# A fused conditional transformer block: the adapter takes two batches at once in halves of the matrix array, and its last bias is added to the tokens by GpSimd

## The chip, the cores and the metric

The kernel runs on one core of one Trainium2 chip. A core has five engines that each work through their own queue in order: TensorE (PE in the profile; its weight loads are shown as PEld), VectorE (DVE), ScalarE (ACT), GpSimd (POOL) and SyncE (SP, which here only issues transfers). Sixteen DMA engines serve all queues. The metric is the device time of one execution in microseconds. The kernel before was timed three times: 921.53, 926.4 and 923.14 us, so its median is 923.14 us.

## The reference, cut to what matters

Four layers follow one another for 16 batches of 256 tokens with 256 features, all in float32. The change touches the first of them, the adapter, which picks one of 16 expert matrices per batch:

```python
# layer 0: adapter (A = 64), x is [16, 256, 256]
hidden = gelu(x @ down_W.T + down_b)                     # [b, 256, 64]
expert = hidden @ expert_W[domain_id].T + expert_b[domain_id]
hidden = where(valid, expert, hidden) + domain_emb[domain_id]
x      = layernorm(hidden @ up_W.T + up_b + x) * gamma + beta
# layer 1: x = ln(x) * (1 + scale(t)) + shift(t); q, k, v; 16 heads of 16
scores = q @ k.T / 4 + attention_bias ; masked ; softmax ; @ v ; @ Wo ; + x
x      = x + (gelu2(ln(x) @ W1 + b1) @ W2 + b2)          # 256 -> 1024 -> 256
# layer 2: one of three small networks, chosen per batch; x = ln(x + net(x))
# layer 3: one step of a Fokker-Planck equation: products with stencils, relu
```

The attention bias (`side` in the kernel) has 16 x 16 x 256 x 256 elements, 64 MB, and is the largest input by far.

## The kernel before, in words

The tokens of a batch lie as 128 partitions by two chunks by 256 features. Every layer is written as a Python generator that goes through the batches and yields where it must wait: `prepare` (the adapter and the first two normalisations), `project` (q, k, v), `weigh` (scores and exponentials, four heads at a time, a "quad"), `attend` (the weights turned by the PE and multiplied with v), `enter` and `feed` (the feed-forward part), `end` (the chosen network), and `step` (the stencils). A small planner, `Flow`, keeps an estimated clock for each engine and for each of seven PSUM banks, and always continues the generator that is ready and has the lowest due time. The due time of a generator starts at a number given in `flow.add` and grows with the PE time that its steps claim, divided by a claimed PE time per batch. So the planner writes out, once, when the program is built, the order of all instructions on all engines; on the chip each engine follows its own list, and waits on semaphores where the data is not there yet.

Of the adapter, `prepare` issues this for each batch b:

- L523: two matmuls that multiply the transposed tokens with `w_down` (the contraction over 256 features in two halves of 128); the result `a_h` has 64 partitions (the adapter's width) by 256 tokens. A float32 matmul leaves two records on the PE, two passes of 256 columns.
- L525: gelu with the bias, by ScalarE, 64 partitions. ScalarE holds one set of function tables at a time, so the gelu needs a table load, and the next exponential needs another one.
- L540 and L542: one 64 x 64 matmul with the batch's expert matrix `e_w`; VectorE adds the chosen expert bias and embedding and writes `hid`, a tile of 65 partitions whose last row is all ones.
- L549 and L550: two matmuls of `hid` with `up`, which has 65 rows: the last one is `up_b`, so the row of ones adds the bias. VectorE adds the result to the tokens.
- Then mean and variance (L407, L408 on VectorE and four small instructions on GpSimd, L411 to L415), the normalisation with gamma and beta (for batch 0 on VectorE, L437 and L440; later on with two GpSimd instructions, L446 and L447), again mean and variance, and the normalised tile `c_ln` (L423 or L428), which `project` turns and multiplies with the weights of q, k and v.

One transfer per batch (L244) brings tokens and transposed tokens together, 512 KB into one of two buffers, and one (L295) brings the expert matrix, whose index SyncE first reads from a tile. Both are issued by `prepare` during the batch before. SyncE's queue also holds the loads of the attention bias: 1 MB per quad in four transfers (L307), three buffers. From batch 1 on, the mask is added to a loaded quad by a GpSimd transfer that accumulates (L508).

At the start, matmuls on zeros (`idle`, L222) stand between the adapter's steps of batches 0 and 1. In the first quads there is no earlier batch whose later layers could fill the PE.

## Time and profile before

| What | Value |
|---|---|
| median of three runs | 923.14 us |
| profiled execution | 919.35 us, of which the span is 917.5 us |
| TensorE clock granted, mean over the span | 0.990 |
| PE / DVE / ACT / POOL busy | 885.9 / 639.5 / 568.6 / 357.1 us |
| adapter matmuls (records, busy): L523, L540, L549 | 64, 18.1 us; 32, 10.3 us; 64, 16.8 us |
| transfers | 163.05 MB, mean 178 GB/s |

The profile comes from one execution. "Busy" is the time in which an engine had at least one instruction of the group under way. Matmuls overlap, so the mean duration of one (380 ns for 256 columns) is longer than the distance from one start to the next; where a price is wanted, the distance between the starts of neighbouring groups in the timeline is the better figure. Idle time is shown with what ended it. A line number is a line of the kernel.

### The profile page before, as it was taken

The page shows a single profiled execution, that of the slowest core. Times are in us where ns is not written, and L with a number is a line of the kernel's source. Part 1 is how long each engine was busy: PE and PEld are TensorE (multiplying, and loading weights), DVE is VectorE, ACT ScalarE, POOL GpSimd, SP SyncE. Part 2 cuts the span into 40 slices and gives each one's busy share as a digit, 9 for nine tenths or more (in the row PEclk, how much of TensorE's full clock was granted, in tenths as well). Part 3 has the DMA queues.
Part 4 walks back from the last instruction along what each step waited for, and adds up shares of the span by engine and source line. Part 5 has one row for each costly group of instructions (what it writes and reads, how often), then busy time and mean ns, then how long its engine had stood idle before and what let it go on. Part 6 is the DMA issues. An engine that isn't in the chain of part 4 may idle for free. (4 is left out here: it accounts for less than half of the span.)

```text
span 917.5 us, 18282 instructions
## 1 busy us (share of the span) xinstructions
PE 885.9 (97%) x6180; PEld 698.2 (76%) x6180; DVE 639.5 (70%) x2110; ACT 568.6 (62%) x1561; POOL 357.1 (39%) x500
## 2 busy tenths in 40 slices
PE   8899998999999999999999999999999999999997
PEld 3567675887777887778788777877887788778885
DVE  6677767767785767677686777768777785766343
ACT  2576667667665766758576675847667576656330
POOL 2233329142632616245261614526161543422331
PEclk8999999999999999999999999999999999999999
DMA  9389887776596767949676794967678486861010
GB/s 292 102 241 326 231 217 193 203 206 184 139 239 171 185 184 183 228 127 242 170 176 179 189 247 114 238 171 170 178 204 208 124 206 173 213 149 42 1 41 24
DMA packets 126555, 163.05 MB, mean 178 GB/s; under 512 B 12455, under 2 KB 86266, under 8 KB 126458
## 3 DMA queue, kind: packets, MB, share of 16 engines
q0 software_dynamic: 31680, 62.92, 34.1%
q1 hardware_dynamic: 93568, 96.92, 32.5%
q10 hardware_dynamic: 1209, 1.99, 0.7%
q8 instruction: 52, 0.85, 0.4%
q14 instruction: 46, 0.37, 0.1%
HBM read 94.69 MB, written 4.19 MB: 108 GB/s over the span
## 5 line engine op out<-in xcount | busy, mean ns | idle before, releaser
L718 ACT ACTIVATE c_pr<-c_sc,c_mx 128x256 f32<-128x256 f32 x512 | 255.1, 500 | 179.6 <-DVE c_mx L707 178.7
L707 DVE CUSTOM_DVE_ANT_0 c_sc<-c_s,side 128x256 f32<-128x256 f32 x512 | 194.4, 417 | 28.3 <-ACT e_o L1096 7.7
L454 PE MATMUL c_pt<-ident,c_pr 128*128 128x128 f32 x1024 | 143.5, 278 | 7.0 <-ACT c_pr L718 5.2
L454 PEld LDWEIGHTS c_pt<-ident,c_pr 128*128 128x128 f32 x1024 | 116.6, 142 | 34.6 <-ACT c_pr L718 12.7
L462 DVE COPY c_pts<-c_pt 128x512 f32<-128x512 f32 x183 | 122.8, 685 | 27.7 <-PE c_pt L454 27.4
L508 POOL DMA_DIRECT2D side<-neg x60 | 80.8, 1355 | 143.9 <-DMA side<-in_side 70.4
L411 POOL TENSOR_SCALAR rs<-mv 128x2 f32<-128x2 f32 x64 | 14.2, 221 | 293.6 <-DVE mv L408 291.7
L873 PE MATMUL d_f<-d_ht,w 128*128 128x256 f32 x512 | 121.4, 381 | 0.1
L903 PE MATMUL d_o<-w,d_z 128*128 128x256 f32 x512 | 116.0, 380 | 0.0
L903 PEld LDWEIGHTS d_o<-w,d_z 128*128 128x128 f32 x512 | 95.0, 190 | 12.3 <-issue 0.4
L873 PEld LDWEIGHTS d_f<-d_ht,w 128*128 128x128 f32 x512 | 92.8, 190 | 11.9 <-issue 0.9
L718 ACT ACTIVATION_READ_ACCUMULATOR c_pr<-c_sc,c_mx 128x1 f32 x512 | 96.1, 188 | 0.0
L689 PE MATMUL c_s<-c_kt,c_qz 32*128 32x256 f32 x1024 | 76.6, 401 | 0.8 <-DVE c_mx L707 0.4
L772 PE MATMUL c_c<-c_pts,c_va 128*32 128x256 f32 x1024 | 72.0, 387 | 3.3 <-DVE c_pts L462 2.9
L689 PEld LDWEIGHTS c_s<-c_kt,c_qz 32*128 32x128 f32 x1024 | 47.9, 184 | 23.5 <-issue 15.8
L892 ACT ACTIVATE d_f<-d_z 128x512 f32<-128x512 f32 x64 | 38.2, 597 | 28.5 <-DVE d_z L889 27.7
L772 PEld LDWEIGHTS c_c<-c_pts,c_va 128*32 128x32 f32 x1024 | 27.5, 109 | 33.4 <-issue 16.1
L911 DVE SCALAR_TENSOR_TENSOR y<-d_o,y 128x256 f32<-128x256 f32 x32 | 13.6, 424 | 55.5 <-PE d_o L903 55.5
L889 DVE TENSOR_SCALAR d_z<-d_f,cols 128x256 f32<-128x256 f32 x102 | 44.5, 477 | 10.7 <-PE d_f L873 9.9
L412 POOL TENSOR_TENSOR rs<-rs,inv_sqrt 128x2 f32<-128x2 f32 x64 | 46.0, 719 | 5.3
L464 ACT COPY c_pts<-c_pt 128x512 f32<-128x512 f32 x73 | 41.7, 572 | 8.8 <-PE c_pt L454 7.7
L896 DVE SCALAR_TENSOR_TENSOR d_z<-d_f,d_z 128x512 f32<-128x512 f32 x64 | 43.1, 673 | 3.5 <-ACT d_f L892 3.5
(152 smaller groups left out, 1602.2 us busy)
## 6 DMA issues: line engine op xcount, KB each, us to landing
side<-in_side SPq DMA_DIRECT2D x256, 256.0 KB, 5.6
side<-neg POOLq DMA_DIRECT2D x60, 1024.0 KB, 8.4
x<-in_x SPq DMA_DIRECT2D x16, 512.0 KB, 5.6
d_w<-in_W_branch SPq DMA_DIRECT2D x16, 512.0 KB, 6.4
out<-e_o SPq DMA_DIRECT2D x15, 256.0 KB, 4.9
w<-in_W SPq DMA_DIRECT2D x2, 1024.0 KB, 7.5
d_bout<-in_bl_branch SPq DMA_DIRECT2D x16, 128.0 KB, 5.8
grids<-in_grids SPq DMA_DIRECT2D x1, 1792.0 KB
```

The costliest lines, as they stand in the source:

```text
L412: nc.gpsimd.tensor_tensor(rs, rs, inv_sqrt, ALU.pow)
L454: nc.tensor.transpose(ps[:, k, c * P : (c + 1) * P], src[:, c, k * P : (k + 1) * P], ident)
L462: nc.vector.tensor_copy(dst, ps)
L508: nc.gpsimd.dma_start(out=sides[m].rearrange("p (h c) k -> p h (c k)", h=HB), in_=negs[m // 4].rearrange("p c k -> p (c k)").unsqueeze(1). ...
L689: nc.tensor.matmul(ps[i][:, c, :], qz[rows32, par, half, c * P : (c + 1) * P], k_t[rows32, half, :], start=b > 0, stop=b > 0 or c == NC - 1,)
L707: nc.vector.tensor_tensor_reduce(out=sc[:, c, :], in0=ps[i][:, c, :], in1=sb[:, i * NC + c, :], scale=-1.0, scalar=3.0e38, op0=ALU.add, op ...
L718: nc.scalar.activation(pr[:, c, :], sc[:, c, :], AF.Exp, bias=mx[:, c : c + 1], scale=-1.0, accum_out=sums[:, c, h : h + 1],)
L772: nc.tensor.matmul(ps_c[32 * i : 32 * i + 32, :], va[:, k, 4 * half + i, 2 * par : 2 * par + 2, :].rearrange("p e d -> p (e d)"), turned[i ...
L873: nc.tensor.matmul(ps_f[:, i, :], w1[:, k, f * P : (f + 1) * P], h_t[:, k, :], start=k == 0, stop=k == NC - 1,)
L889: nc.vector.tensor_scalar(z[:, i, :], ps_f[:, i, :], b1[:, f : f + 1], None, ALU.add)
L896: nc.vector.scalar_tensor_tensor(z, ps_f, 1.0, z, ALU.add, ALU.mult)
L903: nc.tensor.matmul(ps_o, us[f // 2][:, f % 2, c * P : (c + 1) * P], w2[:, f, :], start=f == 0, stop=f == NF - 1,)
```

## The change

The adapter becomes a generator of its own, `adapt`, that goes through eight pairs of batches. Batch 2p uses one half of the array and batch 2p + 1 the other:

- The first product puts the two batches into two halves of the array's columns: both contract over 128 rows and write 64 partitions each, 0 to 63 and 64 to 127 of one tile `p_h`.
- One gelu over 128 partitions serves both batches.
- The expert product of one batch uses rows 0 to 63 and columns 0 to 63, that of the other rows 64 to 127 and columns 64 to 127; one VectorE instruction adds the bias for both.
- The last product uses rows 0 to 63 for one batch and rows 64 to 127 for the other, with `up` held twice, and writes two PSUM banks. Its bias is no longer a row of `up`: it arrives, spread over all partitions, at the end of `rows_a`, and GpSimd adds it to the tokens beforehand (`biased`). The row of ones is gone.

The tokens and the transposed tokens now arrive by transfers of their own (three buffers of 256 KB, and one of 512 KB for a pair, in two transfers). `prepare` waits until its batch is adapted; the other steps of it stay. Two of the `idle` matmul groups, one of 256 columns and one of 512, are gone. The numbers in the `flow.add` calls are others.

```diff
-    def load_x(b):
-        xs[b] = xp.tile([P, NC, 2 * D], F32, name=f"x{b}", tag="x")
+    def load_turned(p):
+        arrives["t", p] = flow.clock["PE"] + 9.0 if p else 0.0
+        xts[p] = xp.tile([P, 2, NC, S], F32, name=f"xt{p}", tag="xt", bufs=1)
+        for i in range(2):
+            nc.sync.dma_start(out=xts[p][:, i], in_=chunked(t["x_t"][2 * p + i]))
+    def load_x(b):
+        arrives["x", b] = flow.clock["PE"] + 7.0 if b > 1 else 0.0
+        xs[b] = xp.tile([P, NC, D], F32, name=f"x{b}", tag="x", bufs=3)
         nc.sync.dma_start(out=xs[b], in_=chunked(t["x"][b]))
-    load_x(0)
-    up = load("up", t["up"], [A + 1, D])
+    load_turned(0)
+    up = load("up", t["up"], [2 * A, D])
...
-    def load_expert(b):
-        e = nc.sync.value_load(e_idx[0:1, b : b + 1], min_val=0, max_val=E + 1)
-        w = xp.tile([A, A], F32, name=f"e_w{b}", tag="e_w")
-        nc.sync.dma_start(out=w, in_=t["expert_W"][bass.ds(e, 1)].rearrange("e a o -> a (e o)"))
-        e_ws[b] = w
+    def load_expert(p):
+        e_ws[p] = xp.tile([2 * A, A], F32, name=f"e_w{p}", tag="e_w")
+        for i in range(2):
+            e = nc.sync.value_load(e_idx[0:1, 2 * p + i : 2 * p + i + 1], min_val=0, max_val=E + 1)
+            nc.sync.dma_start(
+                out=e_ws[p][i * A : (i + 1) * A, :],
+                in_=t["expert_W"][bass.ds(e, 1)].rearrange("e a o -> a (e o)"),
+            )
...
-    rows_a = load("rows_a", rows(t["rows_a"]), [P, 4 * D])
-    ln0_g, ln0_b, bv, bo = (rows_a[:, i * D : (i + 1) * D] for i in range(4))
+    rows_a = load("rows_a", rows(t["rows_a"]), [P, 5 * D])
+    ln0_g, ln0_b, bv, bo, up_b = (rows_a[:, i * D : (i + 1) * D] for i in range(5))
...
+    load_expert(0)
+    load_x(0)
     load_mask(0)
-    load_expert(0)
     load_side(0)
     load_x(1)
-    load_expert(1)
...
+    def biased(b):
+        x = xs[b]
+        nc.gpsimd.tensor_tensor(x, x, up_b.unsqueeze(1).to_broadcast([P, NC, D]), ALU.add)
+        flow.pool(1.35, arrives["x", b])
+        done.add(("x", b))
+
+    def adapt():
+        for p in range(B // 2):
+            yield lambda: p in e_ws
+            yield arrives.get(("t", p), 0.0)
+            parts = [slice(i * A, (i + 1) * A) for i in range(2)]
+            w, xt = e_ws.pop(p), xts.pop(p)
+            ps_h = misc(f"p_h{p}", [2 * A, S])
+            for k in range(NC):
+                for i in range(2):
+                    nc.tensor.matmul(
+                        ps_h[parts[i]], w_down[:, k, :], xt[:, i, k, :], start=k == 0, stop=k == NC - 1
+                    )
+            h1 = xp.tile([2 * A, S], F32, name=f"a_h1{p}", tag="a_h1", bufs=1)
+            nc.scalar.activation(h1, ps_h, AF.Gelu, bias=columns("down_b"))
+            at = free(f"p_h{p}", flow.act(0.47, flow.pe(1.0), "gelu"))
+            if p == 0:
+                expert_bias()
+            yield at
+            if p == 0:
+                spread_mask(0)
+                for b in range(2):
+                    biased(b)
+            ps_e = misc(f"p_e{p}", [2 * A, S])
+            for i in range(2):
+                nc.tensor.matmul(ps_e[parts[i]], w[parts[i]], h1[parts[i]], start=True, stop=True)
+            h2 = xp.tile([2 * A, S], F32, name=f"a_h2{p}", tag="a_h2", bufs=1)
+            nc.vector.tensor_scalar(h2, ps_e, e_add[:, p : p + 1], None, ALU.add)
+            at = free(f"p_e{p}", flow.dve(0.4, flow.pe(0.5)))
+            if p and 2 * p + 2 < B:
+                load_turned(p + 1)
+                load_expert(p + 1)
+            if p:
+                yield lambda: ("x", 2 * p + 1) in done
+            yield at, 2
+            if p == 0:
+                timestep()
+                idle(256)
+            ps_u = [misc(f"p_u{2 * p + i}", [P, NC, D]) for i in range(2)]
+            for c in range(NC):
+                for i in range(2):
+                    nc.tensor.matmul(
+                        ps_u[i][:, c, :], h2[parts[i], c * P : (c + 1) * P], up[parts[i]], start=True, stop=True
+                    )
+            at = flow.pe(1.0)
+            for b in (2 * p, 2 * p + 1):
+                x = xs[b]
+                nc.vector.tensor_tensor(x, ps_u[b % 2], x, ALU.add)
+                adapted[b] = free(f"p_u{b}", flow.dve(0.7, at))
+                done.add(("adapt", b))
+                yield 0.0, 0
+
     def prepare():
         for b in range(B):
-            w = e_ws.pop(b)
-            xx = xs.pop(b)
-            x, xt = xx[:, :, :D], xx[:, :, D:]
...
+            yield lambda: ("adapt", b) in done
+            x, at = xs.pop(b), adapted.pop(b)
+            yield at, 0
+            flow.spent += 0.75
+            if b + 2 < B:
+                load_x(b + 2)
+                if b == 0:
+                    load_turned(1)
+                    load_expert(1)
+            if b == 1:
+                choose()
             stat, at = take_stats(f"0_{b}", x, at)
...
             lns[b] = ln, normalized(ln, x, stat, b == 0)
+            flow.spent += 1.5
+            if b + 2 < B:
+                biased(b + 2)
             done.add(("normal", b))
...
-    flow.add(prepare(), -2.56, 2.25)
-    flow.add(project(), -0.82, 5.7)
+    flow.add(adapt(), -3.55, 1.2)
+    flow.add(prepare(), -2.34, 2.25)
+    flow.add(project(), -0.88, 5.7)
...
-    flow.add(enter(), -0.26, 0.44)
+    flow.add(enter(), -0.11, 0.44)
...
-    flow.add(end(), 2.77, 3.95)
-    flow.add(step(), 4.22, 7.0)
+    flow.add(end(), 2.86, 3.95)
+    flow.add(step(), 4.31, 7.0)
```

## The prediction

> **What bounds the kernel now.** I read the page first, then busy time by stretches of the span, then the waits of the PE, then the timeline around adapter groups and of the first 32 us.
>
> ```profile
> span 917.5 us, 18282 instructions
> PE 885.9 (97%) x6180; PEld 698.2 (76%) x6180; DVE 639.5 (70%) x2110; ACT 568.6 (62%) x1561; POOL 357.1 (39%) x500
> ...
> 10.00:20.00 10.00, 9.09 (x32) 5.01 (x32) 7.15 (x29) 4.59 (x7) 1.99 (x6) 0.76 1.08 363
> ...
> 120.00:160.00 40.00, 35.39 (x263) 26.01 (x265) 30.84 (x106) 27.95 (x79) 25.39 (x33) 0.96 0.79 199
> ...
> 520.00:560.00 40.00, 39.97 (x283) 32.61 (x278) 29.83 (x102) 27.10 (x77) 14.45 (x20) 1.00 0.77 192
> ```
>
> The columns of a stretch are its length, busy time of PE, PEld, DVE, ACT and POOL (with counts), granted clock, DMA share and GB/s. From 160 to 800 us the PE is busy practically without a break (39.97 of 40 us) while DVE has 10 us and POOL 25 us to spare: there, PE time taken out of the queue is time won. Of 31.6 us in which the PE is idle (917.5 - 885.9), about 4 lie before 30 us, 12 from 30 to 160 us, 9 at the end. So two questions decide: how much PE time the pairing removes after the start, and what it does to the start.
>
> The timeline gives the price of the adapter's groups as the distance from a group's start to the next start:
>
> ```profile
> 215.15 1.08 PE L523 MATMUL a_h<-x,w_down 128*64 128x256 f32 x4
> 216.16 0.33 PE L454 MATMUL c_pt<-ident,c_pr 128*128 128x128 f32 x1
> ...
> 220.50 0.64 PE L540 MATMUL a_e<-a_h,e_w 64*64 64x256 f32 x2
> 221.07 0.33 PE L454 MATMUL c_pt<-ident,c_pr 128*128 128x128 f32 x1
> ...
> 184.70 1.15 PE L689 MATMUL c_s<-c_kt,c_qz 32*128 32x256 f32 x16
> 185.78 0.33 PE L454 MATMUL d_t<-ident,d_ln 128*128 128x128 f32 x1
> ...
> 218.91 1.07 PE L772 MATMUL c_c<-c_pts,c_va 128*32 128x256 f32 x16
> 219.91 0.33 PE L454 MATMUL c_pt<-ident,c_pr 128*128 128x128 f32 x1
> ```
>
> Four records of `a_h` take 1.01 us, two of `a_e` 0.57; `a_u` takes 0.96 before a score group (183.74 to 184.70) and 0.87 before a full one (235.14 to 236.01). Sixteen records of scores (four row strips) take 1.08 us and sixteen of `c_c` (four column strips of one bank) 1.00 us: as long as four. Strips do run side by side here, with both passes of float32.
>
> **Change, term 1: PE time after the start.** Per batch before: 1.01 + 0.57 + 0.92 = 2.50 us. Per pair after: `p_h` four slots of two column halves, 1.01 (nearest row `a_h`; `c_c` says 1.00); `p_e` two slots, 0.57; `p_u` four slots of two row halves, 1.08 (nearest row: scores). Together 2.66, against 5.00. I count from the first score group, 30.33 us before. Before, batch 1's `a_u` and batches 2 to 15 come after it: 0.96 + 14 x 2.50 = 36.0 us. In the changed order pair 1's `p_h` and `p_e` stand before batch 0's q, so what follows is its `p_u` and pairs 2 to 7: 1.08 + 6 x 2.66 = 17.0 us. Gain 19.0 us. Bounds: 20.2 if a pair costs one batch's smallest sum (2.45); 16 if halves overlap less well than strips (a half slot of 0.22 us lost at each of some 14 places); nothing if they don't overlap at all (a rival below).
>
> A rule speaks against part of it. The rows show four column strips in one bank at once, but no two row strips in one bank, as `p_e` has them. The Trainium skill, "TensorEngine Tiling (Array Packing)", Restrictions and Gotchas, says that different row tiles cannot access one PSUM bank at the same time. By it `p_e` would cost two slots of 0.22 us more per pair, 2.6 us in six pairs, and the sum at the end would be 915.2.
>
> **Term 2: the start.** The lines that matter:
>
> ```profile
> 11.10 0.48 SPq L295 DMA_DIRECT2D e_w<-in_expert_W  x1
> ...
> 15.09 2.79 SPq L307 DMA_DIRECT2D side<-in_side  x4
> ...
> 19.76 1.97 PE L523 MATMUL a_h<-x,w_down 128*64 128x256 f32 x4
> ...
> 20.54 0.73 DVE L423 TENSOR_SCALAR c_ln<-x,mv,rs 128x256 f32<-128x256 f32 x2 [0.80 <-POOL rs L412]
> ...
> 24.05 0.30 PEld L597 LDWEIGHTS c_q<-c_xt,w_qkv 128*128 128x128 f32 x2 [0.54 <-ACT c_xt L583]
> 24.06 2.02 PE L597 MATMUL c_q<-c_xt,w_qkv 128*128 128x256 f32 x8
> ```
>
> Before, batch 0 reaches q at 24.06, after VectorE wrote `c_ln` at 20.54. In the changed program's order VectorE's queue has the bias addition of pair 1 (it waits for `p_e` of pair 1) directly ahead of batch 0's `c_ln`, and the PE's queue has `p_h` and `p_e` of pair 1 ahead of batch 0's turn `c_t`. Pair 1 needs the transposed tokens of batches 2 and 3, and SyncE issues those after three quads of side data (the last ends at 15.09 + 2.79 = 17.9 before). Ahead of them now stand one more index read and expert transfer (0.8 + 0.5), `x` of batch 0 and the mask (0.4 each), less the expert transfer that stood at 11.10 (1.3): third quad at 18.7, `x` of batch 2 and the two turned loads by 19.9. A load of tokens lands 5.6 us later (median): 25. By bytes: 7.55 MB stand in the two queues up to that load, 6.70 MB had moved by 22.9 us before (292 GB/s, first slice of the page), and 0.35 MB per us was the rate while the DMA was full: 25.3. I take 25.0. Then `p_h` at the slow clock, 1.97 (the row at 19.76; warm 1.08): 27.0; to `p_e` another 0.9 with the gelu (8.60 to 10.57 less 1.08); to VectorE's addition 0.68 (23.33 to 24.01), it takes 0.5; `c_ln` from about 29.1; to q 2.2 more (0.93, then `c_t` 0.64, then `c_xt` 0.61 by the starts at 22.80, 23.44, 24.05): 31.3, or 7.3 later than before.
>
> After the idle matmuls, which end near 20, the PE now stands still until 25. The row at 19.76 shows what a low clock does (1.97 for 1.01; granted 0.76 in that stretch). Whether q and k follow at the low clock costs 0 to 1.9 us (their eight matmuls of 1.89 doubled); 1.2 is taken, as the row nearest is cold. The Trainium skill, "TensorE: Matmul & The Clock Gate", Part 1, says that one idle window of about 3.4 us halves the clock and about 3.4 us of work restore it; by it 1.7 would be lost, and the sum would end at 913.1.
>
> Start: 7.3 + 1.2 = 8.5 us lost. Bounds: 4.9 (tokens at 23.5, every matmul warm) and 11 (landing 6.9 us, the longest shown, and 1.9 for the clock). GpSimd's additions for batches 0 and 1 (its queue has both ahead of the first `rs`) wait for `x` of batch 1, issued near 12, landed near 18 (6.0 to 6.8 in that stretch): `rs` of batch 0 moves from 15.7 to about 21, still ahead of the 29 above, so it costs nothing; if the turned tokens came early it would be next, with `c_ln` near 25.
>
> **Term 3: what lies beside.** GpSimd: 16 additions of 128x512 at 1.27 to 1.60 us (L447, L446): 20 to 26 us in a queue with 560 us idle. Behind each stand the `rs` of the next normalisation and the mask transfers (L508); before, that queue waited 70.4 us for side data alone, and VectorE's reductions waited 4.1 us for the masked data. Cost 0; with that cover gone, 26; no gain, since nothing leaves that queue but two memsets. ScalarE loses 8 gelus of 0.47 and 16 table loads of 1.28 (62 to 46), VectorE 8 additions of 0.47; the planner also shifts evictions between the two, and by the rows DVE ends 14 and ACT 12 us lower. The PE waited 5.2 us for exponentials, 2.9 for turned weights (all before 160 us) and 7.7 for `e_t`; at the start less adapter work is now left to fill such gaps, later less evicting delays them: -5 to +4, taken as 0. SyncE issues 16 more transfers of 0.42, 6.7 us, beside 393 us of waiting for side buffers: 0 after the start. The two `idle` groups (0.7 and 1.3 us) leave a stretch where the PE waits anyway: 0.
>
> **Sum.** 919.35 - 19.0 + 8.5 = 908.9 for an execution like the profiled one, whose span has 1.85 us around it. The median stands 3.79 us above that execution: 912.6.
>
> **Rivals.**
> - *The halves don't overlap.* Then a pair costs 5.0, the gain is nil and the start still costs 8.5: 931.6. For it: no 64-wide pair in the trace. Against: strips of both kinds overlap. 0.04.
> - *The start costs little*, because tokens land early and batch 1's earlier projection fills gaps in which the PE waited for exponentials: 923.14 - 19 = 904. 0.14.
> - *Another engine becomes the bound for part of it*: half of the 19 us turns into PE waiting for DVE or ACT. For it: DVE at 30 of 40 us, waits by 120 to 160 us. 923.14 - 9.5 + 8.5 = 922.1. 0.10.
> - *Slower: GpSimd blocks.* An addition waits for its `x`, whose load stands behind a side load that waited up to 17.0 us for its buffer; the mask transfer behind it comes late, and with it the scores' reduction on VectorE. It decides from 10.5 / 14 = 0.75 us of PE wait per addition; at 1.6 us each the time is 912.6 + 22 = 935. Against: `x` is loaded one batch earlier than it is added, some 50 us. 0.09.
>
> **Numbers.** The forecast itself has 0.63. Its own range, by the bounds: 919.35 - 20.2 + 4.9 - 5 = 899 and 919.35 - 16 + 11 + 4 = 918, plus 3.8: 903 to 922. It holds the second rival and, stretched to 923, the third; together 0.8 or a little more, since some of the first 0.63 may fall outside. Half a per cent, 4.6 us, is about what a measurement tells from no change: faster means under 918.5. Faster: 0.58 + 0.14 + 0.02 = 0.74; same 0.05 + 0.07 + 0.02 = 0.14; slower 0.04 + 0.07 + 0.01 = 0.12.
>
> **What would show it.** Right: `p_h`, `p_e`, `p_u` groups of eight, four and eight records with two starting together, 1.0, 0.6 and 1.1 us to the next group; first q near 31 us, with `c_ln` just after pair 1's bias; PE busy near 863 us; 39.9 of 40 us in the middle. Wrong: records one after the other; q near 25; new PE waits that lead to `x` on GpSimd; middle stretches under 39 us.

## The result and the profile after

The changed kernel takes 923.22 us (median of 12 runs, 917.59 to 927.28) where the kernel before takes 923.86 (12 runs, 920.27 to 926.4): a ratio of 0.999 with a 95% interval of 0.9966 to 1.0014. The forecast was 912.6, so nothing is seen of the 10.5 us that the change should have given. The spread of the runs goes with the granted clock of TensorE: its mean was 0.985 in the run of 917.59 us and 0.974 in that of 927.28, and 0.011 of the span is 10 us. The profiled execution of the changed kernel took 923.92 us, about its median; that of before lies 4.5 us under its own. A difference between the two traces is therefore some 5 us too large.

The head of the page, and stretches of the span in the columns of the prediction (length, busy time of PE, PEld, DVE, ACT and POOL with counts, granted clock, DMA share, GB/s), of the changed kernel:

```profile
span 922.1 us, 18224 instructions
PE 882.4 (96%) x6180; PEld 692.1 (75%) x6180; DVE 627.8 (68%) x2078; ACT 556.5 (60%) x1561; POOL 376.6 (41%) x514
...
10.00:20.00 10.00, 7.63 (x29) 4.93 (x28) 3.54 (x14) 4.61 (x7) 4.04 (x3) 0.60 1.06 335
20.00:30.00 10.00, 7.95 (x20) 3.31 (x20) 3.73 (x13) 0.47 (x1) 4.14 (x9) 0.50 0.62 189
30.00:40.00 10.00, 8.41 (x24) 6.29 (x23) 5.20 (x22) 2.17 (x5) 1.35 (x4) 0.54 0.27 83
...
280.00:320.00 40.00, 37.78 (x275) 29.69 (x274) 26.23 (x94) 25.52 (x74) 14.96 (x18) 1.00 0.76 191
520.00:560.00 40.00, 39.85 (x282) 31.83 (x283) 27.36 (x91) 28.35 (x76) 17.60 (x23) 1.00 0.74 188
720.00:760.00 40.00, 37.40 (x286) 29.37 (x285) 27.11 (x87) 24.88 (x71) 14.75 (x16) 1.00 0.81 203
```

The same stretches of the kernel before, as far as they aren't shown above:

```profile
20.00:30.00 10.00, 9.92 (x42) 6.75 (x42) 4.71 (x20) 4.33 (x8) 0.92 (x3) 0.90 0.46 134
30.00:40.00 10.00, 7.75 (x52) 4.89 (x54) 7.46 (x27) 4.56 (x17) 2.94 (x6) 0.83 0.00 1
...
280.00:320.00 40.00, 39.70 (x290) 32.60 (x284) 28.76 (x99) 24.01 (x70) 21.31 (x30) 1.00 0.72 183
720.00:760.00 40.00, 39.70 (x298) 31.96 (x298) 29.89 (x102) 28.46 (x82) 19.95 (x26) 1.00 0.81 204
```

TensorE is 3.5 us less busy than before, not some 23 (863 was forecast). The granted clock is 0.50 to 0.60 from 10 to 40 us, where before had 0.76, 0.90 and 0.83. In the middle two stretches fall under 38 of 40 us; the kernel before had 39.70 in both.

The timeline of the new adapter groups (start, busy time, engine, line, operation, records), each with the group behind it:

```profile
361.56 1.08 PE L543 MATMUL p_h<-xt,w_down 128*64 128x256 f32 x8
362.58 0.66 PE L464 MATMUL c_pt<-ident,c_pr 128*128 128x128 f32 x4
...
106.76 0.65 PE L558 MATMUL p_e<-a_h,e_w 64*64 64x256 f32 x4
107.34 0.33 PE L464 MATMUL c_pt<-ident,c_pr 128*128 128x128 f32 x1
...
310.45 1.13 PE L574 MATMUL p_u<-up,a_h 64*128 64x256 f32 x8
311.51 0.50 PE L738 MATMUL c_s<-c_kt,c_qz 32*128 32x256 f32 x4
```

From start to start the three take 1.02, 0.58 and 1.06 us for two batches: the halves do run side by side, at the prices that the prediction took from the scores and from one batch. The saving itself is real.

The start, on TensorE and VectorE:

```profile
25.91 2.65 PE L543 MATMUL p_h<-xt,w_down 128*64 128x256 f32 x8 [1.48 <-DMA xt<-in_x_t]
29.13 1.12 PE L558 MATMUL p_e<-a_h,e_w 64*64 64x256 f32 x4 [0.56 <-ACT a_h L547]
31.18 1.22 PE L464 MATMUL c_t<-ident,c_ln 128*128 128x128 f32 x4 [0.94 <-DVE c_ln L433]
33.06 3.78 PE L646 MATMUL c_q<-c_xt,w_qkv 128*128 128x256 f32 x8 [0.66 <-ACT c_xt L632]
36.63 3.19 PE L646 MATMUL c_k<-c_xt,w_qkv 128*128 128x256 f32 x8
39.66 1.89 PE L689 MATMUL c_v<-w_qkv,c_xt 128*128 128x256 f32 x8
...
42.36 0.93 PE L738 MATMUL c_s<-c_kt,c_qz 32*128 32x256 f32 x12
...
30.32 0.48 DVE L560 TENSOR_SCALAR a_h<-p_e,e_add 128x256 f32<-128x256 f32 x1 [5.49 <-PE p_e L558]
30.72 0.73 DVE L433 TENSOR_SCALAR c_ln<-x,mv,rs 128x256 f32<-128x256 f32 x2
```

The kernel before, at the same places:

```profile
25.91 1.89 PE L597 MATMUL c_k<-c_xt,w_qkv 128*128 128x256 f32 x8
...
30.33 1.15 PE L689 MATMUL c_s<-c_kt,c_qz 32*128 32x256 f32 x16
```

The chain is the one predicted, with `c_ln` directly behind pair 1's bias addition, but later and slower. The first q starts at 33.06 us (24.06 before, 31.3 forecast), q and k take 3.78 and 3.19 us (2.02 and 1.89 before), and the first score group starts at 42.36 us (30.33 before): 12.0 us are lost where 8.5 were expected.

So 12.0 us are lost at the start. From the first score group to the end of the span the two traces need 887.2 and 879.8 us, so there the change wins 7.4 us by the traces. By the medians, which are equal, it wins about 12, if the starts in these two executions are the usual ones. The adapter's own TensorE time there fell from 36.6 us to 19.2 (distances from start to start), by 17.4. Two questions remain: is the start carried to the end, and where did the other 5 us (10 by the traces) go?

The changed kernel's four longest waits of TensorE from 43 to 880 us (waiting operation, what it waited for, total us, times, longest):

```profile
PE c_s L738 <- DVE c_mx L756: 3.8, 2, 3.1
PE c_pt L464 <- DVE x L580: 2.1, 1, 2.1
PE c_c L821 <- ACT c_pts L474: 1.8, 1, 1.8
PE c_pt L464 <- ACT c_qz L665: 1.5, 1, 1.5
```

In the whole list no matmul waits for GpSimd, and no row has more than three waits in the 16 batches. These waits look like places where an order of work happens to be unlucky.

### The profile page after: what moved, and what is told of

It is laid out like the page before. It is cut to its first block, busy times and chain, and to the rows that moved or that the text cites. A ratio compares the mean times of both kernels' runs of the same rounds, so it can differ in the third digit from the quotient of the medians.

```text
span 922.1 us, 18224 instructions
## 1 busy us (share of the span) xinstructions
PE 882.4 (96%) x6180; PEld 692.1 (75%) x6180; DVE 627.8 (68%) x2078; ACT 556.5 (60%) x1561; POOL 376.6 (41%) x514
## 5 line engine op out<-in xcount | busy, mean ns | idle before, releaser
L472 DVE COPY c_pts<-c_pt 128x512 f32<-128x512 f32 x175 | 117.2, 685 | 26.8 <-PE c_pt L464 26.5
L952 PEld LDWEIGHTS d_o<-w,d_z 128*128 128x128 f32 x512 | 94.9, 190 | 12.5 <-DVE c_mx L756 0.6
L474 ACT COPY c_pts<-c_pt 128x512 f32<-128x512 f32 x81 | 45.5, 575 | 21.1 <-PE c_pt L464 21.0
L456 POOL TENSOR_TENSOR b_tmp<-b_tmp,rows_a 128x512 f32<-128x512 f32 x15 | 19.6, 1304 | 84.1 <-DVE b_tmp L433 65.7
L938 DVE TENSOR_SCALAR d_z<-d_f,cols 128x256 f32<-128x256 f32 x88 | 38.5, 479 | 17.3 <-PE d_f L922 17.2
```

The source lines that it names most:

```text
L472: nc.vector.tensor_copy(dst, ps)
L474: nc.scalar.copy(dst, ps)
L938: nc.vector.tensor_scalar(z[:, i, :], ps_f[:, i, :], b1[:, f : f + 1], None, ALU.add)
L952: nc.tensor.matmul(ps_o, us[f // 2][:, f % 2, c * P : (c + 1) * P], w2[:, f, :], start=f == 0, stop=f == NF - 1,)
```

## The experiments

The theories. *Work:* a microsecond of TensorE work removed is a microsecond won. *Cover:* part of the removed matmuls stood where TensorE would have waited for VectorE or ScalarE, so a part is never won. *GpSimd:* its 16 additions delay others. *Start:* what is lost before the first scores is lost at the end. *Order:* how the remaining work is interleaved is worth as much as the change. The kernel writes its order while it is built: a planner keeps a clock for each engine from fixed costs, and of the chains that can go on it takes the one with the smallest progress, which begins at an offset and advances at a pace given in its `flow.add` call. Where I speak of the planner's clock, I mean its TensorE clock after the last step, a number of the program and not of the chip.

### TensorE work taken out, or added, in an unchanged order

The kernel before, with two matmuls of four fewer in `a_h` and `a_u`:

```diff
-            for k in range(NC):
-                nc.tensor.matmul(ps_h, w_down[:, k, :], xt[:, k, :], start=k == 0, stop=k == NC - 1)
+            nc.tensor.matmul(ps_h, w_down[:, 0, :], xt[:, 0, :], start=True, stop=True)
...
-            for c in range(NC):
-                nc.tensor.matmul(ps_u[:, c, :], h2[:, c * P : (c + 1) * P], up, start=True, stop=True)
-            nc.vector.tensor_tensor(x, ps_u, x, ALU.add)
+            nc.tensor.matmul(ps_u[:, 0, :], h2[:, :P], up, start=True, stop=True)
+            nc.vector.tensor_tensor(x, ps_u[:, 0:1, :].to_broadcast([P, NC, D]), x, ALU.add)
```

> The kernel before, its instruction order untouched, with two matmuls per batch left out: the second half of the adapter's first contraction, and the second half of its last product (VectorE adds the first half's result to both chunks of tokens). The output is therefore not the reference's. It takes 4 slots of 0.216 us per batch off the PE, 12.5 us after the first score group (batch 1's last product and batches 2 to 15). Theory 'PE time is time': the execution gets about 12 us shorter, 0.987. Rival 'the other engines' pace comes to light': PE time taken out returns largely as PE waits in the middle of the span, since the changed kernel took 17.4 us of work out there and won 7.4; then some 5 us are won, 0.994.

Measured: 916.54 us, ratio 0.9929 (0.9904 to 0.9954). 12.5 us of work left after the first scores, and 7.0 of 923.56 were won: 56%, or between 34 and 71% by the interval.

The changed kernel, with the groups of `p_h` and `p_u` of pairs 2 to 7 issued twice:

```diff
...
+            if p > 1:
+                for k in range(NC):
+                    for i in range(2):
+                        nc.tensor.matmul(
+                            ps_h[parts[i]], w_down[:, k, :], xt[:, i, k, :], start=k == 0, stop=k == NC - 1
+                        )
...
+            if p > 1:
+                for c in range(NC):
+                    for i in range(2):
+                        nc.tensor.matmul(
+                            ps_u[i][:, c, :], h2[parts[i], c * P : (c + 1) * P], up[parts[i]], start=True, stop=True
+                        )
```

> The changed kernel, order untouched, with the first and the last product of pairs 2 to 7 done twice over (same values written again). It puts 8 slots of 0.216 us per pair back, 10.4 us in all after the start. 'PE time is time': 10 us longer, 1.011. 'Other engines' pace': the added time fills waits that are there anyway, 2 to 5 us longer, 1.002 to 1.005.

Measured: 930.98 us, ratio 1.0074 (1.0047 to 1.0102), 7.8 us above the changed kernel for 10.4 us of work: 75%. By the two intervals the 7.8 are known to some 3 us, so this run alone would also admit the whole 10.4.

The first run excludes that the whole counts, and the second agrees with it. At 56 to 75% of TensorE time, 17.4 us are worth 10 to 13, and about 12 were won by the medians. *Work* falls.

### GpSimd's additions left out

```diff
-        nc.gpsimd.tensor_tensor(x, x, up_b.unsqueeze(1).to_broadcast([P, NC, D]), ALU.add)
-        flow.pool(1.35, arrives["x", b])
+        flow.pool(1.35, arrives["x", b])
```

> The changed kernel without GpSimd's 16 additions of the last bias (the bias is left out of the result), order of everything else untouched. If GpSimd's longer queue makes the new waits in the middle, 5 to 10 us shorter; if it lies beside other work, as predicted, within 2 us of the changed kernel. At the start nothing is expected, since there the first q waits for the turned tokens of batches 2 and 3.

Measured: 921.82 us, ratio 0.9979 (0.9958 to 0.9999). About 1.4 us below the changed kernel, known to some 3 us and so not resolved from nothing: of 16 additions of about 1.27 us, 20 in all, most is hidden. The 5 to 10 us that *GpSimd* needs aren't there, so it falls.

### The start

First, pair 1 held back in the planner until batch 0's projection stands:

```diff
         for p in range(B // 2):
+            if p == 1:
+                yield lambda: ("prepare", 0) in done
```

> The changed kernel; pair 1 of the adapter is held back until batch 0's k is issued, so that neither VectorE's queue nor the PE's has pair 1 ahead of batch 0's first normalised tile. Theory 'the start is lost for good': batch 0's q starts near 28 us instead of 33 and the first scores near 36.5 instead of 42.4, and the whole gets about 6 us shorter. Rival 'the start is made up later, the middle sets the time': the first scores come earlier by as much but the end moves by less than 2 us.

Measured: 931.2 us, ratio 1.0091 (1.0057 to 1.0125). The first scores came at 38.56 us, 3.8 earlier than in the changed kernel, and the end 8 us later. The planner had written another order for everything that follows, so this was no test of the start; it was the first sign of *order*.

Then only SyncE's order was changed, and that of the other engines kept: pair 1's tokens right behind `p_h` of pair 0 instead of behind three quads of side data.

```diff
-    load_side(0)
     load_x(1)
...
-    load_side(1)
-    wo = load("wo", chunked(t["Wo"]), [P, NC, D], engine=nc.sync)
-    load_side(2)
+    side_at.update((m, 6.5) for m in range(3))
+    wo = fixed("wo", [P, NC, D])
+    early = {}
+
+    def load_first():
+        load_turned(1)
+        load_expert(1)
+        early["t"], early["w"] = xts.pop(1), e_ws.pop(1)
+        load_side(0)
+        load_side(1)
+        nc.sync.dma_start(out=wo, in_=chunked(t["Wo"]))
+        load_side(2)
...
+            if p == 0:               # in adapt, behind p_h
+                load_first()
...
-                    load_turned(1)
-                    load_expert(1)
+                    arrives["t", 1] = flow.clock["PE"] + 9.0
+                    xts[1], e_ws[1] = early["t"], early["w"]
```

> The changed kernel with transfers alone in another order: SyncE issues the turned tokens and the expert matrices of pair 1 right after p_h of pair 0, ahead of the first three quads of side data and Wo; the order of the instructions on TensorE, VectorE, ScalarE and GpSimd is that of the changed kernel, and all is computed. All theories: the tokens of pair 1 land near 17 us instead of 25, c_ln of batch 0 comes near 23 instead of 30.7, the first q near 25.5 instead of 33.1, the first score group near 32 instead of 42.4. Theory S (the start cost 12 us and all of it is carried to the end): 10 us faster than the changed kernel, 913 us, ratio to the kernel before 0.989. Theory O (the lost time is that of the order after the start, and a late start is mostly made up later by TensorE having more work ready): no more than 3 us faster than the changed kernel, 920 or more, ratio 0.996 or more. In between, say 917, each has about half.

Measured: 917.89 us, ratio 0.9942 (0.992 to 0.9965). The first scores came at 37.44 us, 4.9 earlier, and the time fell by 5.3, known to some 3 us. So what this start gained arrived at the end, as closely as this can be told, but it gained half of what I had expected, since two other things came next, as its VectorE and TensorE timelines show:

```profile
16.85 0.69 DVE L590 TENSOR_TENSOR x<-p_u,x 128x512 f32<-128x512 f32 x1 [2.75 <-POOL x L537]
18.07 0.69 DVE L590 TENSOR_TENSOR x<-p_u,x 128x512 f32<-128x512 f32 x1 [0.53 <-POOL x L537]
...
28.28 3.78 PE L656 MATMUL c_q<-c_xt,w_qkv 128*128 128x256 f32 x8 [0.66 <-ACT c_xt L642]
31.85 3.06 PE L656 MATMUL c_k<-c_xt,w_qkv 128*128 128x256 f32 x8
...
37.44 0.93 PE L748 MATMUL c_s<-c_kt,c_qz 32*128 32x256 f32 x12
```

VectorE waits for GpSimd's additions at the start, and q and k still run at the half clock. For the former, I put x of batches 0 and 1 and the mask ahead of the expert matrices, and the additions ahead of the mask on GpSimd:

```diff
-    load_expert(0)
     load_x(0)
-    load_mask(0)
     load_x(1)
+    load_mask(0)
+    load_expert(0)
...
-                spread_mask(0)
                 for b in range(2):
                     biased(b)
+                spread_mask(0)
```

> The changed kernel with the tokens of pair 1 ahead of the side data, as in the run that came to 917.9 us, and besides with x of batches 0 and 1 and the mask issued before the expert matrices, and GpSimd's two bias additions put ahead of its work on the mask; the order on TensorE, VectorE and ScalarE is that of the changed kernel, and all is computed. There VectorE waited 2.75 and 0.53 us for x from GpSimd at 16.9 and 18.1 us. Theory S (a microsecond of the start is a microsecond of the end): first score group 1.5 to 4 us earlier than 37.4, time 914 to 916.5. Theory O (the start is made up later): 917 to 918.5.

Measured: 918.58 us, ratio 0.9939 (0.992 to 0.9958), the same as without. I had expected an earlier start, and it came 2.4 us later (first scores at 39.83): the expert matrices now stood behind x, and `p_e` of pair 0 waited 3.19 us for them. That the time stayed the same speaks against *start*, if anything, but the difference of the two times is known to some 2.5 us only, so the run decides nothing.

### The order of the work

The changed kernel, with the offsets of the kernel before for five chains:

```diff
-    flow.add(prepare(), -2.34, 2.25)
-    flow.add(project(), -0.88, 5.7)
+    flow.add(prepare(), -2.56, 2.25)
+    flow.add(project(), -0.82, 5.7)
...
-    flow.add(enter(), -0.11, 0.44)
+    flow.add(enter(), -0.26, 0.44)
...
-    flow.add(end(), 2.86, 3.95)
-    flow.add(step(), 4.31, 7.0)
+    flow.add(end(), 2.77, 3.95)
+    flow.add(step(), 4.22, 7.0)
```

> The changed kernel with the planner's starting offsets for the projection, the entry, the branch and the last step put back to those of the kernel before (by 0.06 to 0.15 us); nothing that is computed changes, only the order. Theory N (an order's details are worth several us either way, whatever the change): the time differs from the changed kernel's 923.2 by 2 us or more. Theory F (an order's details average out): within 1.5 us of it, ratio 0.998 to 1.001.

Measured: 948.62 us, ratio 1.0285 (1.0251 to 1.0318). Steps of 0.06 to 0.22 in five numbers cost 25 us. The kernel before with less work, from above, in an order written for that work, said the same:

```diff
-            at = free(f"a_h{b}", flow.act(0.47, flow.pe(0.9), "gelu"))
+            at = free(f"a_h{b}", flow.act(0.47, flow.pe(0.47), "gelu"))
...
-            at = free(f"a_u{b}", flow.dve(0.7, flow.pe(0.9)))
+            at = free(f"a_u{b}", flow.dve(0.7, flow.pe(0.47)))
...
-    flow.add(prepare(), -2.56, 2.25)
+    flow.add(prepare(), -2.56, 1.39)
```

> The kernel before with two matmuls less in every batch (the second half of a_h's contraction, and the second half of a_u, whose first half is added to both halves of the tokens: both left out of the computation), as in the run that took 12.5 us of TensorE time out after the start and won 7; here the planner is told the smaller costs (0.47 for 0.9 us twice, a new step every 1.39 us instead of 2.25) and writes another order. Theory P (the removed time was not all won because the order was written for the old costs): 911 us, ratio 0.9865. Theory C (the adapter's matmuls cover waits for VectorE and ScalarE wherever they stand, so some 60 per cent is won in any order): 916.5, ratio 0.993, with the lines of TensorE's waits as spread as before. If the order itself is worth several us either way, it may land above 919.

Measured: 966.01 us, ratio 1.0453 (1.0425 to 1.0481), 49 us above the same work in the old order.

So I looked for other offsets and paces by the planner's clock, for both kernels with the same effort. The changed kernel with pair 1's tokens first, and the best set found for it:

```diff
-    flow.add(adapt(), -3.55, 1.2)
-    flow.add(prepare(), -2.34, 2.25)
-    flow.add(project(), -0.88, 5.7)
-    flow.add(weigh(), 0, 21.2)
-    flow.add(attend(), 0.96, 11.3)
-    flow.add(enter(), -0.11, 0.44)
-    flow.add(feed(), 2.45, 13.9)
-    flow.add(end(), 2.86, 3.95)
-    flow.add(step(), 4.31, 7.0)
+    flow.add(adapt(), -4.088, 1.2212)
+    flow.add(prepare(), -2.43, 2.2554)
+    flow.add(project(), -0.923, 5.6375)
+    flow.add(weigh(), -0.136, 24.5226)
+    flow.add(attend(), 0.946, 11.3159)
+    flow.add(enter(), -7.057, 0.3576)
+    flow.add(feed(), 2.461, 13.9461)
+    flow.add(end(), 2.777, 3.9697)
+    flow.add(step(), 4.191, 7.0037)
```

> The kernel with the tokens of pair 1 first (917.9 us), with other starting offsets and paces for the planner's nine chains, under which the planner's own clock ends at 875.6 instead of 889.9; nothing that is computed changes. Theory O (what the change won after the start is set by the order of the work, which the planner's own clock foretells, as it put the order with the old offsets 37.6 us later and the chip 25): 6 to 14 us faster than 917.9, so 904 to 912. Theory C (the removed matmuls were cover for VectorE and ScalarE, and no order wins the rest): 915 to 921.

Measured: 904.93 us, ratio 0.9782 (0.9762 to 0.9802), 13 us below the same start in the old order. Its page head and three of its stretches:

```profile
span 903.3 us, 18233 instructions
PE 870.1 (96%) x6180; PEld 687.5 (76%) x6180; DVE 632.4 (70%) x2086; ACT 554.9 (61%) x1553; POOL 377.4 (42%) x514
...
280.00:320.00 40.00, 39.30 (x278) 31.57 (x277) 29.90 (x99) 25.73 (x73) 19.91 (x26) 1.00 0.76 192
520.00:560.00 40.00, 40.00 (x294) 31.95 (x293) 29.00 (x98) 25.32 (x71) 14.50 (x24) 1.00 0.65 171
720.00:760.00 40.00, 40.00 (x311) 32.10 (x312) 27.24 (x95) 26.51 (x75) 8.16 (x14) 1.00 0.72 186
```

The stretches that had 37.78 and 37.40 are full or nearly so, and TensorE, with the same 6180 records, is 12 us less busy. Half of that is the clock: by its steps in the two traces, TensorE was busy at half clock for 35.7 us in the changed kernel and for 23.5 here, which is worth some 6 us. The rest is a lesson in reading: short pauses between matmuls count as busy. I therefore took the distance between the starts of two matmul records that follow each other, less the distance that the same two (by tiles, shapes and place in their groups) do not exceed in the fastest 15 of 100 cases over all profiled kernels, and summed this excess from 45 to 880 us. It is 38 us in the kernel before, 52 in the changed one, 75 with the old offsets, 36 here, and 48 in the kernel before with less work, where time taken out came back as pauses. (Against the kernel before these sums may be some 5 us too large, since its profiled execution was a quick one.) Of the 14 us that the changed kernel has more than the kernel before, 5.7 show as idle time of TensorE (21.6 against 15.9), and some of it is half clock in this stretch too (10.2 us busy at it, against 2.9). So the 5 to 10 us after the start that are missing went into pauses, seen and unseen, and into the clock; the new order has no more excess than the kernel before.

The same offsets with the changed kernel's own transfers, so that only the `flow.add` lines above differ from it:

> The changed kernel with its own transfers (side data ahead of pair 1's tokens), and only the planner's nine offsets and paces put to those of the run that came to 904.9 us. Theory S and O add: the start costs the 5.3 us that it cost with the old order, 910.2. If the new order absorbs a late start: 905 to 907. If the order needs the early start: 915 or more.

Measured: 907.91 us, ratio 0.9825 (0.9805 to 0.9845), with first scores at 41.4 us. Nine lines of offsets are worth 15 us to the changed kernel as it stood. Against the run before this one, the late start costs 3.0 us, known to some 2.5, for 3.6 us of delay: *start* holds here as well.

The new offsets with x early (the start of the miss above):

> The changed kernel with both: the transfers and GpSimd's order of the run with x early, and the offsets under which the planner's clock ends at 875.6; all is computed. Theory S and O together: the gains add, 902 to 909. If the new order starts late anyway, or the two gains overlap: 909 to 914.

Measured: 908.15 us, ratio 0.9814 (0.9794 to 0.9834): 3 us worse than without, in keeping with that start (first scores at 39.80, 2.0 us later).

A second set for the changed kernel with tokens first, found from another beginning:

```diff
...
+    flow.add(adapt(), -4.195, 1.2614)
+    flow.add(prepare(), -2.318, 2.2651)
+    flow.add(project(), -0.887, 5.6232)
+    flow.add(weigh(), -0.236, 22.8358)
...
```

> The changed kernel with pair 1's tokens first and a second set of offsets, found in the same way from another beginning; the planner's clock ends at 879.1 (875.6 for the first set, 889.9 for the old one). Theory O (the planner's clock foretells it for the changed kernel): 904.9 + 3.5 = 908, between 905 and 913. If the first set was one lucky order: 914 to 922.

Measured: 905.54 us, ratio 0.9801 (0.978 to 0.9823). The first set was no single lucky order.

Now the kernel before, with three other sets, of which the third lies close to its own:

```diff
...
+    flow.add(prepare(), -2.606, 2.256)      # first set
+    flow.add(project(), -0.604, 5.7119)
+    flow.add(weigh(), -0.046, 27.1271)
...
+    flow.add(prepare(), -2.485, 2.2613)     # second set
+    flow.add(project(), 0.749, 5.9676)
+    flow.add(weigh(), -4.387, 24.1486)
...
+    flow.add(prepare(), -2.579, 2.25)       # third set
+    flow.add(project(), -0.872, 5.7)
+    flow.add(weigh(), -0.079, 21.2)
...
```

> The kernel before with other starting offsets and paces for its eight chains, under which the planner's own clock ends at 889.0 instead of 901.3, found with the same effort as for the changed kernel; nothing that is computed changes. Theory O: the kernel before gains as much by it, 6 to 12 us, 911 to 917, and the changed kernel's lead under equal effort is what the planner's clocks say, 13.4 less the late start. Theory C: within 3 us of 923.5.

> The kernel before with a second set of offsets, found in the same way from another beginning; the planner's clock ends at 890.0 (889.0 for the first set, which came to 925.0 on the chip, and 901.3 for its own). If the first set was an unlucky order for the kernel before: 911 to 917. If TensorE's own work holds the kernel before where it is, so that its best orders are about as good as its own: 919 to 927.

> The kernel before with offsets close to its own (the largest step is 0.08), under which the planner's clock ends at 893.3 instead of 901.3. If the kernel before can gain by its order as the changed one did: 914 to 919. If its own order is about as good as any found: 921 to 927.

Measured: 924.95 us, ratio 1.0001 (0.998 to 1.0021); 926.24, ratio 1.0025 (1.0011 to 1.0038); 916.81, ratio 0.9917 (0.9889 to 0.9945). The planner's clock had promised 11 to 12 us for the first two and 8 for the third, so in steps of this size it is no measure of the chip, though it foretold the bad order with the old offsets (927.6 against 889.9); and the kernel before, too, had 6 to 8 us lying in its order.

| kernel | offsets | planner's clock | measured us |
|---|---|---|---|
| before | own | 901.3 | 923.9 |
| before | first, second, third set | 889.0, 890.0, 893.3 | 925.0, 926.2, 916.8 |
| changed | own | 889.9 | 923.2 |
| changed | those of before | 927.6 | 948.6 |
| changed | first set | 875.6 | 907.9 |
| changed, tokens first | own | 889.9 | 917.9 |
| changed, tokens first | first, second set | 875.6, 879.1 | 904.9, 905.5 |

Is TensorE's work, then, the whole bound in a good order? The kernel of 904.93 us with `p_h` and `p_u` of pairs 2 to 7 issued twice, by the edit shown above:

> The run of 904.9 us with p_h and p_u of pairs 2 to 7 issued twice: 6 x (1.0 + 1.06) less the mode switch already paid, 10 to 12 us more on TensorE; nothing is left out. With the old order the same cost 7.8 of 10.4 us. Theory O (the new order has TensorE waiting less, so its work counts in full): 9.5 to 12 us more, 915 to 917. Theory C (a quarter or more of it is still cover for VectorE and ScalarE): 6 to 8.5 us more, 911 to 913.5.

Measured: 912.01 us, ratio 0.9866 (0.9847 to 0.9886), 7.1 us more for 10.4 (in the trace the twelve doubled groups take 1.88 and 1.93 us, the single ones 1.01 and 1.06): 68%, known to some 3 us. So *cover* probably holds in the new order as in the old one, with about a third of the work standing where TensorE would wait anyway, but this run alone does not exclude that the whole counts. *Order* and *cover* can both be true; they are not rivals.

### The low clock at the start

Three more matmuls on zeros, where TensorE stood still for 0.58, 0.93 and 0.66 us:

```diff
+            if p == 1:
+                idle(512)        # in adapt, behind p_h
...
+            if p == 1:
+                idle(512)        # in adapt, behind p_e
...
+            if b == 0:
+                idle(512)        # in project, behind the turn of c_ln
```

> The run of 904.9 us with three more idle matmuls of 512 columns on TensorE: after p_h of pair 1, after p_e of pair 1 and after the turn of batch 0, where TensorE stood still 0.58, 0.93 and 0.66 us and the granted clock was 0.50 through q and k; all else is the same, and all is computed. If standing still is what took the clock down there and the start is carried to the end: q and k at 2.0 and 1.9 us instead of 3.78 and 3.10, first scores 2 to 3 us earlier than 37.8, time 902 to 903.5. If the clock stays down all the same: the three cost their length at half clock, first scores 1 to 2 us later, 905 to 907.

Without them (the kernel of 904.93 us), by stretches and in the timeline:

```profile
24.00:28.00 4.00, 2.44 (x16) 0.90 (x12) 1.69 (x8) 0.48 (x2) 1.07 (x3) 0.93 0.99 314
28.00:32.00 4.00, 3.40 (x8) 2.77 (x9) 3.47 (x14) 1.01 (x2) 1.49 (x2) 0.50 0.35 101
...
25.48 0.65 PE L568 MATMUL p_e<-a_h,e_w 64*64 64x256 f32 x4 [0.58 <-ACT a_h L557]
27.07 0.88 PE L472 MATMUL c_t<-ident,c_ln 128*128 128x128 f32 x4 [0.93 <-DVE c_ln L441]
28.61 3.78 PE L656 MATMUL c_q<-c_xt,w_qkv 128*128 128x256 f32 x8 [0.66 <-ACT c_xt L642]
...
37.81 1.15 PE L748 MATMUL c_s<-c_kt,c_qz 32*128 32x256 f32 x16
```

With them, by stretches and in the timeline:

```profile
24.00:28.00 4.00, 4.00 (x18) 1.47 (x16) 1.59 (x7) 0.47 (x1) 0.72 (x4) 0.97 0.97 312
28.00:32.00 4.00, 4.00 (x18) 2.91 (x17) 3.79 (x15) 1.02 (x2) 1.27 (x1) 1.00 0.31 95
...
28.74 1.98 PE L662 MATMUL c_q<-c_xt,w_qkv 128*128 128x256 f32 x8
30.55 1.89 PE L662 MATMUL c_k<-c_xt,w_qkv 128*128 128x256 f32 x8
...
34.97 1.15 PE L754 MATMUL c_s<-c_kt,c_qz 32*128 32x256 f32 x16
```

With the three waits filled the clock stays at full, so standing still was what took it down, and the first scores come at 34.97 instead of 37.81 us. Without them it fell near 27.8 us (0.95 was granted from 26 to 28), behind the first two waits and ahead of the third, so the first two were enough. The time is 903.72 us, ratio 0.9786 (0.9761 to 0.981), against 0.9782 without. The 2.8 us at the start are seen, but whether they reach the end is not resolved. A single trace is also no exact measure of a start: the kernel with `p_h` and `p_u` issued twice has the same instructions as that of 904.93 us up to 45 us, and had its first scores at 39.71. These two kernels, of 903.72 and 904.93 us, are the fastest of the study, some 19 us under the kernel before.

## Why the prediction was wrong

**The halves overlap** (term 1): right, 1.02, 0.58 and 1.06 us against 1.01, 0.57 and 1.08. The rival in which they don't falls. The rule from the Trainium skill, "TensorEngine Tiling (Array Packing)", Restrictions and Gotchas, that different row tiles cannot access one PSUM bank at the same time, cost nothing here: `p_e` writes one bank, in separate partitions, from two row halves and takes 0.58 us, where one batch's `a_e` took 0.57.

**PE time after the start** (term 1): forecast 19.0 us, measured 17.4; 1.6 us too much. The prices of the groups were right; but pair 1's `p_u` ran at half clock (2.01 us to the next start), and behind three of the six `p_e` the next group came late (0.98 us).

**PE time taken out is time won** (the first reading, "practically without a break"): this is the step that failed. A busy time of 39.97 of 40 us hid short pauses. In an unchanged order 56 to 75% of TensorE work counts, and of 17.4 us about 12 were won by the medians. TensorE's waits for VectorE and ScalarE, put between -5 and +4 and taken as 0, are the term that should have had about +5. It is the largest part of the miss of 10.6 us; the start has 3.5 of it, the PE time 1.6, and 0.7 is the median of before, 923.14 us in three runs and 923.86 in twelve. The rival "another engine becomes the bound for part of it", given 0.10, came nearest in number (922.1) and in kind, though no engine's speed is the limit, since another order of the same work takes 15 us off. That its number came so near is luck: it had 3.5 us too little for the start and lost 9.5 us of TensorE's time where about 5 were lost.

**The start** (term 2): the mechanism was right in each link, the size was not. The tokens let `p_h` start at 25.91 us instead of 25.0; `p_h` took 2.65 us instead of 1.97; q came at 33.06 instead of 31.3. The clock cost 3.0 us from q to the first scores (9.30 for 6.27), where 1.2 was taken and 1.9 was the upper bound, since q and k both ran at half the clock. Together 12.0 against 8.5, beyond the bound of 11. I had priced one cold group behind one standstill: "their eight matmuls of 1.89 doubled" is one group, and q and k are two. The profile has a clock of 0.50 from 12 to 38 us.

**GpSimd** (term 3): right within what the run tells; its additions are worth 1.4 us, known to some 3, and the rival that it blocks, by 22 us, falls.

**The order**: the prediction followed the queues closely at the start and took the planner's order after it as given. That the new order had other waits of its own had no term and no rival. Runs that change only offsets move the changed kernel by -15 and +25 us. So the equal times of the two kernels are the sum of a saving of 17.4 us, of which by the point values a quarter to two fifths did not count, a start 12 us late, and two orders that each were one of many.

What stays open: what the change is worth apart from its order. The best orders that I found, with the changed kernel's own transfers, stand at 907.9 against 916.8 us, 8.9 us apart, and nothing says that they are equally good. The missing 5 to 10 us after the start are also not divided here between cover, unlucky order and half clock.

## What to carry to other kernels

A kernel whose order is written by a planner is one draw from many orders; before a change of some ten microseconds is judged, a few orders of both versions should be timed. A TensorE at 39.9 of 40 us busy is not TensorE at its limit: add or remove a known piece of work and see which share of it counts. What a change does to the first 40 us should be priced by itself, clock included. Three changes of the start here showed at the end at about their size (4.9 us as 5.3, 3.6 as 3.0, 2.0 as 3.2), and two, of 2.4 and 2.8 us, were not resolved there.

## What the runs showed of the hardware

The low clock lasted longer than the busy time alone would suggest. In the changed kernel TensorE was busy for all of 14 to 24 us and the granted clock stayed at 0.50; part of that work were sixteen records of 16 columns. The clock came back after 4.7 to 6.2 us of wide matmuls: those from 19.64 us on in the kernel of 904.93 us brought it back near 24.4 (0.91 was granted from 24 to 26), q and k from 33.06 on in the changed kernel near 39.2 (0.69 from 38 to 40).

In every trace here the granted clock changes only at times that lie whole multiples of about 3.41 us apart: it is down from 11.95 to 39.26 us in the changed kernel, eight such steps, and from 14.13 to 24.37 in that of 904.93 us, three. In the latter the wide matmuls filled the last step before the rise; in the changed kernel those from 20.66 to 24.4 us filled neither of the steps that they touched (18.78 to 22.19 and 22.19 to 25.60). That fits a clock which rises at the end of a step that was filled with wide work, but no run tests it. The Trainium skill, "TensorE: Matmul & The Clock Gate", Part 1, gives a window of about 3.4 us that runs free of the kernel's start, and one busy or one idle window for a change; the 4.7 and 6.2 us agree with its figure, by which the way up would take one to two windows (3.4 to 6.8 us, an estimate). On the way down the runs show more: the clock fell near 27.8 us at the end of a step in which TensorE was busy for 1.9 of 3.41 us, behind waits of 0.58 and 0.93 us.
